# An image without feed-forward goes first, the weights' signs are made in layer 1's attention, and q is scaled where it is copied

## The chip, the cores and the metric

The kernel runs on one core of one Trainium2 chip. The metric is the device time of a launch in microseconds; the kernel before takes 2424.64 us (median of three runs, 2422.13 to 2425.38). Inside the core, TensorE (PE) multiplies matrices into PSUM, of which this kernel's pool `ps_o` has eight tiles of one bank each; VectorE (DVE), ScalarE (ACT) and GpSimd (POOL) do the rest, and SyncE (SP), ACT and POOL issue the DMAs. Every engine has its own queue of instructions.

## The reference, cut to what matters

The input is eight images of 32 x 32 positions (1024 tokens) and 384 channels, in fp32.

- Layer 0: x = x + attention(group_norm(x)) with six heads of 64. q, k and v come from one weight matrix `qkv_w`; the scores are (q/8)·k plus two relative-position terms, which are products of the unscaled q with two small tables.
- Layer 1: t = t + causal attention(layer_norm(t)), one head of 384.
- Then t = t + feed-forward(layer_norm(t)). Its weights W1 and W2 are replaced by the signs of (w - mean of w's group), in five groups, and its activations are quantised by group over the batch. With eight images and five groups the group size is 8 // 5 = 1, so images 0 to 4 have a feed-forward and for images 5, 6 and 7 that term is zero.

```
gs = n // NUM_GROUPS                       # 8 // 5 = 1
for g in range(NUM_GROUPS):                # images 0..4; the rest stay zero
    ...
Wb = Wb.at[g*gs:(g+1)*gs].set(sign(wg - wg.mean()))
```

## The kernel before, in words

`run` takes the images one after the other, 0 to 7. For each image:

- `layer0` normalises (already done), computes q and k for three pairs of heads (`project_qk`, L435; the copies out of PSUM with the bias are L462 on DVE and L464 on ACT), the relative terms (`positions`, L480 to L497: a table product, a store to DRAM and gathered loads back; `place`, L510 to L518: a split into two parts and DMAs into the tiles `f_r`), and v (`values`, L530).
- `attend0_fast` goes over three pairs p, each with 16 units of scores in six bursts of 2, 3, 3, 3, 3 and 2. A unit is two pairs of score products (L585, L589), one exponential per half (L595, ACT) and, one burst later, the product with v (L606, PE) and the running sum of the probabilities (`f_sum`, L603, DVE). When the sums of a pair are complete, two transposes and two reductions on DVE make `few` (L629, L630); in burst 2 of the next pair `divide` makes the denominators (`f_den`, L638, PE, a PSUM bank), and DVE reads them (L614, L424). In burst 1 of pair 1 the residual x is loaded (L106) and the bias added on POOL (L567).
- `attention1` has the layer norm, q (L763), v (L383) and eight chunks c of causal attention (scores L806, mask L811 on DVE, exponential L813, values L819, and L820 to L822 on DVE). The next image's group norm is done in it.
- `ffn`, for images 0 to 4, reads the sign weights from DRAM (`sign_weights`, L892 to L895, POOL's queue) and does two products (L925, L966). The first two q products of the next image are made inside it (the dictionary `ahead`). An image without feed-forward is followed at once by the next image's q products.

The first image has extra work. `load_weights` loads the weights; L136 multiplies the q part of `wqkv_sb` by 1/8 on ACT, in the queue ahead of the first group norm's square root (L343). `join_biases` (L285) and `multiply_out` (L299, copies L300 on DVE) are products made once. And the generator `binarize` makes the signs: it loads W1 and W2 in three pieces (`f_w`, L229, on POOL's queue), sums them by group (L247, DVE, 20 reductions), gets the means (L255, POOL), loads the pieces again (`f_sign`), turns each into signs (L269 and L270, DVE, 30 of each) and stores them to DRAM (L277, SP). It is advanced step by step by `next(...)`: once per burst in the first image's `attend0_fast` until the first piece's signs are done (the residual waits for that in this image), and then in its `attention1`.

The program fixes the order in which work is written down; the framework's scheduler then lays it out for each engine and may put independent instructions earlier in a queue. Buffers come from rotating pools: eleven image-sized ones (`image_`, from which `f_w` and `f_sign` are taken too), twelve pages for the probabilities, eight PSUM banks. A tile's first write waits until the earlier user of its buffer is done.

Of the kernel before, what the change touches and what calls it, by code (L numbers as in the profile page):

```python
# [31 lines left out]
QB, QEPS = 128.0, 1e-5  # L32
GSB = B // NG
B_FFN = NG * GSB
MASKED = -3.0e38
BURSTS = (2, 3, 3, 3, 3, 2)
BURSTS_AT = [sum(BURSTS[:i]) for i in range(len(BURSTS))]
# [38 lines left out]
def conv_attn_hybrid(  # L76
# [42 lines left out]
    def load_weights(pools):  # L119

        nc.scalar.dma_start(out=bqk, in_=qkv_b[0 : 2 * C].rearrange("(m p) -> p m", p=P))
        nc.vector.memset(rel, 0.0)
        for half in range(2):
            nc.scalar.dma_start(out=rel[half * HD : (half + 1) * HD, 0, : 2 * H - 1], in_=rel_hT)
            nc.scalar.dma_start(out=rel[half * HD : (half + 1) * HD, 1, : 2 * W - 1], in_=rel_wT)
        nc.scalar.dma_start(out=bv, in_=qkv_b[2 * C : 3 * C].rearrange("(m p) -> p m", p=P))
        nc.scalar.dma_start(out=b1_sb, in_=b1.rearrange("(m p) -> p m", p=P))
        src = qkv_w.rearrange("(p k) o -> p k o", k=NC)
        for i in range(3):
            nc.sync.dma_start(out=wqkv_sb[:, :, ts(i, C)], in_=src[:, :, ts(i, C)])  # L130
        nc.sync.dma_start(out=wproj_sb, in_=proj_w.rearrange("(k p) o -> p k o", p=P))
        nc.sync.dma_start(out=pb, in_=proj_b.partition_broadcast(P))
        nc.sync.dma_start(out=wv_sb, in_=wv.rearrange("(k p) o -> p k o", p=P))
        nc.sync.dma_start(out=b2_sb, in_=b2.partition_broadcast(P))

        nc.scalar.mul(wqkv_sb[:, :, 0:C], wqkv_sb[:, :, 0:C], qscale)  # L136
        nc.scalar.mul(bqk[:, 0:NPAIR], bqk[:, 0:NPAIR], qscale)
        nc.scalar.mul(rel, rel, 1.0 / qscale)
        early = pools.small.tile([P, 1], F32, tag="early", name="early_root")
        nc.scalar.activation(early, ones[:, 0:1], AF.Sqrt)  # L140
# [9 lines left out]
    )  # L150

    fold = const.tile([P, 2, 32], F32, name="fold")
    for i in range(2):
        nc.vector.tensor_reduce(fold[:, i, :], ident.rearrange("p (k i) -> p i k", k=4), AX.X, ALU.add)
    ones = const.tile([P, HD], F32, name="ones")
    nc.gpsimd.memset(ones, 1.0)

# [61 lines left out]
    def binarize(pools):  # L219

        def pieces(name):
            for n, piece in enumerate(PIECES):
                room, at = pools.flat(f"{name}_{n}"), 0
                for i, (which, src, sign, k0, k1, n_out) in enumerate(piece):
                    w = room[:, at : at + (k1 - k0) * n_out].rearrange("p (k o) -> p k o", o=n_out)
                    at += (k1 - k0) * n_out
                    nc.gpsimd.dma_start(out=w, in_=src.rearrange("(k p) o -> p k o", p=P)[:, k0:k1, :])  # L229
                    yield which, w, sign[:, k0 * n_out : k1 * n_out], n_out, i + 1 == len(piece)  # L230

        def one_ahead(loads):

            got = next(loads)
            for load in loads:
                yield got
                got = load
            yield got

        part = const.tile([P, 2, 2, NG], F32, name="sums_w")  # L240
        times = [0, 0]
        loads = one_ahead(pieces("w"))
        got = next(loads)
        yield False
        for which, w, _, n_out, _ in itertools.chain([got], loads):
            for g in range(NG):
                nc.vector.tensor_reduce(  # L247
                    part[:, times[which], which, g : g + 1], w[:, :, ts(g, n_out // NG)], AX.XY, ALU.add
                )
            times[which] += 1  # L250
            if which == 1 or w.shape[1] > 1:
                yield False
        nc.vector.tensor_tensor(part[:, 0], part[:, 0], part[:, 1], ALU.add)
        mean = const.tile([P, 2, NG], F32, name="mean_w")
        nc.gpsimd.partition_all_reduce(  # L255
            mean.rearrange("p a g -> p (a g)"), part[:, 0].rearrange("p a g -> p (a g)"), P, bass_isa.ReduceOp.add
        )
        for which, n in enumerate((FF // NG * C, C // NG * FF)):
            nc.vector.tensor_scalar_mul(mean[:, which], mean[:, which], 1.0 / n)
        done = 0  # L260
        for which, w, dst, n_out, last in one_ahead(pieces("sign")):
            gs = n_out // NG
            step = min(C // gs, w.shape[1])
            for k in range(0, w.shape[1], step):
                for g in range(NG):
                    wg, m = w[:, k : min(k + step, w.shape[1]), ts(g, gs)], mean[:, which, g : g + 1]
                    above = pools.xn.tile([P, C], F32, tag="xn", name=f"above_{which}_{n_out}")
                    above = above[:, : wg.shape[1] * gs].rearrange("p (k o) -> p k o", o=gs)
                    nc.vector.tensor_scalar(above, wg, m, None, ALU.is_gt)  # L269
                    nc.vector.scalar_tensor_tensor(wg, wg, m, above, ALU.is_lt, ALU.subtract, reverse1=True)  # L270
                    done += wg.shape[1] * gs
                    if done > 600:
                        done = 0
                        yield False
            if NG * gs < n_out:
                nc.vector.memset(w[:, :, NG * gs :], 0.0)
            nc.sync.dma_start(out=dst.bitcast(F32), in_=w.rearrange("p k o -> p (k o)"))  # L277
            if last:
                yield True
# [22 lines left out]
    def stages(pools):  # L302
# [137 lines left out]
        def layer0(b, xT):  # L440
# [9 lines left out]
            def queries_keys(m):  # L450
# [3 lines left out]
                for half, ps in enumerate(made):  # L454
                    t = ts(half, 512)
                    if m < NPAIR:
                        dst = q[:, p, t]
                    else:
                        dst = k[:, p, t].rearrange("d (g n i) -> d g i n", n=2, i=P)
                        ps = ps.rearrange("d (g i n) -> d g i n", n=2, i=P)  # L460
                    if half:
                        nc.vector.tensor_scalar_add(dst, ps, bias)  # L462
                    else:
                        nc.scalar.activation(dst, ps, AF.Identity, bias=bias)  # L464

# [68 lines left out]
            for m in range(2 * NPAIR):  # L536
# [3 lines left out]
                if m == NPAIR and unfinished:  # L540
# [1 line left out]

                    early = pools.small.tile([P, 1], F32, tag="early", name=f"early0_{b}")
                    nc.scalar.activation(early, k[:, 0, T - 1 :], AF.Exp, scale=0.0)
            if pools.fast and b == 0:
                signs.append(binarize(pools))
                next(signs[0])
            for j in range(NJ):
                values(j)
            for _ in place(0, *near[0]):  # L550
# [7 lines left out]
            later = others()  # L558
            for _ in () if pools.fast else later:
                pass  # L560
            if pools.fast and b == 0:
                join_biases(pools)

            def residual():
# [7 lines left out]
        def attend0_fast(residual, b, q, k, r, v, later):  # L572
# [90 lines left out]
            for p in range(NPAIR):  # L663
                sums = [pools.page(f"sum0_{b}_{p}_{half}") for half in range(2)]
                for n, burst in enumerate(bursts):
                    prs = [scores(p, *u) for u in burst]
                    if b == 0 and (p, n) == (0, 1):
                        multiply_out(pools)
                    for u in pending:
                        values(*u)  # L670
                    if n == 0:
                        if p > 0:
                            few = set_aside(p - 1, *last)
                        avs = [pools.o_tile(f"av0_{b}_{p}_{half}") for half in range(2)]
                    if b == 0 and xt is None and next(signs[0]) or b > 0 and (p, n) == (1, 1):
                        xt = residual()
                    if p == 0:
                        with tc.issue_after(last_exp[0]):
# [76 lines left out]
        def attention1(xt, more, b, between, start):  # L755
# [24 lines left out]
                values(j)  # L780
            for m in range(NC):
                queries(1, m)
                for work in signs:
                    next(work, None)
            for j in range(4, NJ):
                values(j)

# [5 lines left out]
        def attend1_fast(xt, b, q, xT, v, other, start):  # L793
# [33 lines left out]
            for c in range(NJ):  # L827
# [3 lines left out]
                    next(work, None)  # L831
                if c >= 2:
                    values(c - 2)
            for work in signs:
                assert next(work, None) is None
            signs.clear()
            start()
            values(NJ - 2)
            values(NJ - 1)
# [60 lines left out]
        def ffn(xt, b, gn):  # L900

            xs = [pools.halves(f"{n}_{b}", F32R) for n in ("lnT_2", "lnlo_2")]
            for half in range(2):
# [3 lines left out]
                    yield  # L907
                if half == 0 and gn is not None and pools.fast:
                    with tc.issue_after(last_transpose[0]):
                        ahead[b + 1, 0] = project_qk(b + 1, gn, 0)  # L910

            early = pools.small.tile([P, 1], F32, tag="early", name=f"early_{b}")
            nc.scalar.activation(early, rs[:, 0:1], AF.Gelu)
# [24 lines left out]
                            )  # L938
            s, _ = absmax_scale(am.rearrange("p i n -> p (i n)"), f"1_{b}")
            if gn is not None and pools.fast:  # L940
                ahead[b + 1, 1] = project_qk(b + 1, gn, 1)

# [40 lines left out]
        unfinished = []  # L985

        def run(pools):
            gn = load_T(0)
            if pools.fast:
                load_weights(pools)  # L990
            for _ in group_norm_T(0, gn):
                pass
            if pools.fast:
                make_unit(pools)
            for b in range(B):
                xt, more = layer0(b, gn)

                def between():

                    if b + 1 < B:  # L1000
                        yield from group_norm_T(b + 1)

                started = []

# [10 lines left out]
                def finish(b=b, xt=xt, add=add):  # L1015
# [1 line left out]
                        add()  # L1017
                    dst = out[b].rearrange("(j p) c -> p j c", p=P)
                    for q in range(4):
                        (nc.gpsimd if b + 1 < B else nc.sync).dma_start(  # L1020
                            out=dst[:, 2 * q : 2 * q + 2, :], in_=xt[:, 2 * q : 2 * q + 2, :]
                        )

# [52 lines left out]
```

## Time and profile before

| | |
|---|---|
| median of the three runs | 2424.64 us (2422.13 to 2425.38) |
| profiled execution, its span on the core | 2422.6 us; no other time is given for it |
| PE busy | 2378.5 us (98%) |
| DVE busy | 1392.1 us (57%) |
| ACT busy | 1035.4 us (43%) |
| POOL busy | 264.9 us (11%) |
| moved by DMA | 169.98 MB, 70 GB/s on average |

A stretch of the profile is read with the same stretch of another image beside it: all images run the same matmuls in `layer0` and `attention1`, so where the first image takes longer than the seventh, the difference is what its extra work and its waits cost. "Releaser" is what the profile gives as the end of a wait. The granted clock is TensorE's, as a share of full speed.

### The profile page before, as it was taken

What the parts mean: (1) busy time and instruction counts of PE and PEld (TensorE: products, weight loads), DVE (VectorE), ACT (ScalarE), POOL (GpSimd) and SP (SyncE); (2) the same over time, 40 slices, a digit from 0 to 9 for tenths busy, and PEclk for the clock granted to TensorE, in tenths of its full rate; (3) what the DMA queues carried; (4) which work ended last, traced back from release to release, by engine and by line L of the source; (5) the groups of instructions that cost most, each with busy time, mean ns of one, the idle gap of its engine ahead of it and who ended that gap; (6) DMA issues with size and microseconds to landing.
All of it is one profiled execution on the core that took longest, in us unless ns stands there. A gap on an engine that the chain in (4) does not pass through costs nothing.

```text
span 2422.6 us, 25725 instructions
## 1 busy us (share of the span) xinstructions
PE 2378.5 (98%) x9378; PEld 1274.1 (53%) x9378; DVE 1392.1 (57%) x2182; ACT 1035.4 (43%) x1756; POOL 264.9 (11%) x389
## 2 busy tenths in 40 slices
PE   6899999999999999999999999999999999999998
PEld 2434576445774356843458634577435543554354
DVE  4497456773466654557645577346674357525751
ACT  2352265632465513755227463246542155125520
POOL 1220001300013000032000130001300030002100
PEclk9899999999999999999999999999999999999999
DMA  7722205410127011081110631013600270018000
GB/s 196 201 96 79 78 1 121 114 53 14 39 66 170 27 40 39 1 188 64 49 39 1 131 105 65 1 39 86 149 27 1 70 165 27 0 47 161 28 1 28
DMA packets 154793, 169.98 MB, mean 70 GB/s; under 512 B 113408, under 2 KB 126048, under 8 KB 153120
## 3 DMA queue, kind: packets, MB, share of 16 engines
q1 hardware_dynamic: 134416, 98.93, 17.1%
q0 software_dynamic: 17184, 69.22, 9.6%
q8 instruction: 77, 1.26, 0.2%
q10 hardware_dynamic: 3056, 0.08, 0.1%
q14 instruction: 60, 0.49, 0.1%
HBM read 75.38 MB, written 42.47 MB: 49 GB/s over the span
## 4 chain that ended last, share of the span: by engine, by line
PE 96%; DVE 2%; DMA 1%; issue 0%; ACT 0%; POOL 0%; DVEq 0%; ACTq 0%
PE f_s L585 14%; PE f_av L606 14%; PE f_qk L435 10%; PE f_s L806 8%; PE f_av L819 8%; PE f_y L966 7%; PE f_y L925 7%; PE f_v L383 5%; PE f_v L530 5%; PE f_q L763 5%; PE f_s L589 4%; PE f_pj L383 3%; PE f_rel L480 2%; PE f_pj L693 2%; PE f_pt L311 1%; PE f_pj L698 1%
## 5 line engine op out<-in xcount | busy, mean ns | idle before, releaser
L595 ACT ACTIVATE f_pr<-f_s 128x512 f32<-128x512 f32 x768 | 412.1, 595 | 327.2 <-PE f_s L589 287.8
L585 PE MATMUL f_s<-f_q,f_k 64*128 64x512 f32 x1536 | 413.2, 609 | 10.4 <-DVE wqk L300 8.3
L603 DVE TENSOR_TENSOR f_sum<-f_sum,f_pr 128x1024 f32<-128x1024 f32 x288 | 360.8, 1300 | 18.6 <-ACT f_pr L595 18.2
L606 PE MATMUL f_av<-f_pr,f_v 128*64 128x512 f32 x1536 | 363.9, 607 | 0.0
L589 PE MATMUL f_s<-f_r,unit 64*128 64x512 f32 x768 | 309.9, 794 | 0.0
L435 PE MATMUL f_qk<-f_gnT,wqkv_sb 128*128 128x512 f32 x576 | 257.4, 600 | 8.4 <-DVE f_gnT L346 8.4
L585 PEld LDWEIGHTS f_s<-f_q,f_k 64*128 64x128 f32 x1536 | 137.9, 186 | 179.0 <-issue 105.4
L606 PEld LDWEIGHTS f_av<-f_pr,f_v 128*64 128x64 f32 x1536 | 98.9, 137 | 220.6 <-issue 194.3
L806 PE MATMUL f_s<-f_q,f_lnT 128*128 128x512 f32 (+3 forms) x576 | 195.9, 488 | 0.0
L819 PE MATMUL f_av<-f_v,f_pr 128*128 128x385 f32 x576 | 195.3, 486 | 0.0
L435 PEld LDWEIGHTS f_qk<-f_gnT,wqkv_sb 128*128 128x128 f32 x576 | 108.0, 191 | 150.0 <-issue 139.2
L813 ACT ACTIVATE f_pr<-f_s 128x512 f32<-128x512 f32 (+3 forms) x96 | 47.1, 491 | 264.1 <-DVE f_s L811 215.4
L819 PEld LDWEIGHTS f_av<-f_v,f_pr 128*128 128x128 f32 x576 | 108.2, 190 | 77.3 <-issue 11.5
L518 POOL DMA_DIRECT2D f_r<-f_far x192 | 101.2, 530 | 410.3 <-DVE f_far L511 343.5
L806 PEld LDWEIGHTS f_s<-f_q,f_lnT 128*128 128x128 f32 x576 | 102.0, 190 | 77.8 <-issue 54.1
L929 ACT ACTIVATE f_h<-f_y,b_sb 128x256 f32<-128x256 f32 x240 | 100.8, 471 | 67.5 <-PE f_y L925 67.0
L763 PE MATMUL f_q<-f_lnT,wqk 128*128 128x512 f32 x288 | 127.5, 592 | 0.0
L936 DVE TENSOR_REDUCE am<-f_h 128x1 f32<-128x1024 f32 (+2 forms) x80 | 71.6, 946 | 96.4 <-ACT f_h L929 96.4
L383 PE MATMUL f_v<-wv_sb,f_lnT 128*128 128x384 f32 x384 | 126.5, 486 | 0.0
L530 PE MATMUL f_v<-wqkv_sb,f_gnT 128*128 128x384 f32 x384 | 125.1, 486 | 0.0
L589 PEld LDWEIGHTS f_s<-f_r,unit 64*128 64x128 f32 x768 | 75.2, 187 | 91.1 <-issue 89.8
L530 PEld LDWEIGHTS f_v<-wqkv_sb,f_gnT 128*128 128x128 f32 x384 | 75.3, 196 | 50.3 <-issue 3.5
(162 smaller groups left out, 2986.2 us busy)
## 6 DMA issues: line engine op xcount, KB each, us to landing
f_far<-f_far SPq DMA_DIRECT2D x48, 512.0 KB, 3.4
f_r<-f_far POOLq DMA_DIRECT2D x192, 128.0 KB, 4.4
f_r<-f_far SPq DMA_DIRECT2D x192, 128.0 KB, 3.7
f_gnT<-in_xT SPq DMA_DIRECT2D x24, 512.0 KB, 4.7
f_x<-in_x SPq DMA_DIRECT2D x32, 384.0 KB, 5.8
out_y<-f_x POOLq DMA_DIRECT2D x28, 384.0 KB, 4.6
f_near<-f_far SPq DMA_DIRECT2D x128, 64.0 KB, 4.3
f_w1a<-w1s POOLq DMA_DIRECT2D x5, 1536.0 KB, 6.9
```

The source lines that it names most:

```text
L383: nc.tensor.matmul(ps[:, :C], xT[:, k, ts(j, P)], w[:, k, cols], start=(k == 0), stop=(k == NC - 1))
L435: nc.tensor.matmul(made[half], wqkv_sb[:, i, ts(m, P)], xT[:, i, ts(half, 512)], start=(i == 0), stop=(i == NC - 1))
L530: nc.tensor.matmul(ps, keys[:, i, j // 2, j % 2], wqkv_sb[:, i, 2 * C :], start=(i == 0), stop=(i == NC - 1))
L585: nc.tensor.matmul(sc[par], k[rows[par], p, ts(c, P)], q[rows[par], p, ts(half, 512)], start=True, stop=False)
L589: last_score[0] = nc.tensor.matmul(sc[par], unit[rows[par], c // 2 % 2].rearrange("i h w -> i (h w)"), r[2 * (c // 4) + c % 2][rows[par], ...
L595: last_exp[0] = nc.scalar.activation(pr[:, ts(par, 512)], sc[par], AF.Exp).ins
L603: nc.vector.tensor_tensor(sums[half], prev, pr, ALU.add)
L606: nc.tensor.matmul(avs[half][ts(par, HD), :], v[:, c, ts(h, HD)], pr[:, ts(par, 512)], start=(c == 0), stop=(c == NJ - 1),)
L763: nc.tensor.matmul(ps, wqk[:, k, ts(m, P)], xT[:, half, k, :], start=(k == 0), stop=(k == NC - 1))
L806: nc.tensor.matmul(sc[:, lo:], xT[:, c // 4, k, ts(c % 4, P)], q[:, half, k, lo:], start=(k == 0), stop=(k == NC - 1),)
L819: nc.tensor.matmul(av[:, : C + 1], prs[c][:, ts(j - c, P)], v[:, c, :], start=(c == 0), stop=(c == j))
L925: nc.tensor.matmul(ps, w1k[i // 2][:, ts(m, P)], xs[i % 2][:, half, i // 2, :], start=(i == 0), stop=(i == 2 * NC - 1))
```

## The change

Three edits.

1. The order of the images is 5, 0, 1, 2, 3, 4, 6, 7 (`ORDER`, with `AFTER` for the successor). All that was bound to image 0 as the first is bound to image 5; there are as many images with and without feed-forward, and the last one is still 7.
2. `binarize` starts in burst 3 of pair 2 of the first image, and is advanced two steps in each of the eight chunks of `attention1` of image 5 and then of image 0, where it must be finished. Its sums give way after every second group. The residual of the first image is loaded in burst 1 of pair 1 as in every other.
3. The weights of q are no longer multiplied by 1/8 (L136 is gone); the copies of q from PSUM multiply and add the bias in one instruction. The two reductions that make the constant `fold` (L154) are written after the first group norm.

```diff
+ORDER = (B_FFN, *range(B_FFN), *range(B_FFN + 1, B))
+AFTER = dict(zip(ORDER, ORDER[1:]))
...
-        nc.scalar.mul(wqkv_sb[:, :, 0:C], wqkv_sb[:, :, 0:C], qscale)
...
-    for i in range(2):
-        nc.vector.tensor_reduce(fold[:, i, :], ident.rearrange("p (k i) -> p i k", k=4), AX.X, ALU.add)
+
+    def make_fold():
+        for i in range(2):
+            nc.vector.tensor_reduce(fold[:, i, :], ident.rearrange("p (k i) -> p i k", k=4), AX.X, ALU.add)
...
                     part[:, times[which], which, g : g + 1], w[:, :, ts(g, n_out // NG)], AX.XY, ALU.add
                 )
+                if g % 2:
+                    yield False
             times[which] += 1
-            if which == 1 or w.shape[1] > 1:
-                yield False
...
+                    scale = qscale if m < NPAIR else 1.0
                     if half:
-                        nc.vector.tensor_scalar_add(dst, ps, bias)
+                        nc.vector.tensor_scalar(dst, ps, scale, bias, ALU.mult, ALU.add)
                     else:
-                        nc.scalar.activation(dst, ps, AF.Identity, bias=bias)
+                        nc.scalar.activation(dst, ps, AF.Identity, bias=bias, scale=scale)
...
-            if pools.fast and b == 0:
-                signs.append(binarize(pools))
-                next(signs[0])
...
-                    if b == 0 and (p, n) == (0, 1):
+                    if b == ORDER[0] and (p, n) == (0, 1):
                         multiply_out(pools)
+                    if b == ORDER[0] and (p, n) == (2, 3):
+                        signs.append(binarize(pools))
+                        next(signs[0])
...
-                    if b == 0 and xt is None and next(signs[0]) or b > 0 and (p, n) == (1, 1):
+                    if (p, n) == (1, 1):
                         xt = residual()
...
                 queries(1, m)
-                for work in signs:
-                    next(work, None)
...
-            for work in signs:
-                assert next(work, None) is None
-            signs.clear()
+            if b < B_FFN:
+                for work in signs:
+                    assert next(work, None) is None
+                signs.clear()
...
-                        ahead[b + 1, 0] = project_qk(b + 1, gn, 0)
+                        ahead[AFTER[b], 0] = project_qk(AFTER[b], gn, 0)
...
             if pools.fast:
                 make_unit(pools)
-            for b in range(B):
+                make_fold()
+            for b in ORDER:
```

The remaining lines of the diff put `ORDER[0]` and `AFTER[b]` where `0` and `b + 1` stood.

More of the change, by code (lines that the diff above doesn't have):

```diff
@@ L560, in layer0 @@
                 pass
-            if pools.fast and b == 0:
+            if pools.fast and b == ORDER[0]:
                 join_biases(pools)
@@ L940, in ffn @@
             if gn is not None and pools.fast:
-                ahead[b + 1, 1] = project_qk(b + 1, gn, 1)
+                ahead[AFTER[b], 1] = project_qk(AFTER[b], gn, 1)
             def activate(j, m0, m1):
@@ L987, in run @@
         def run(pools):
-            gn = load_T(0)
+            gn = load_T(ORDER[0])
             if pools.fast:
                 load_weights(pools)
-            for _ in group_norm_T(0, gn):
+            for _ in group_norm_T(ORDER[0], gn):
                 pass
@@ L994, in run @@
                 make_unit(pools)
-            for b in range(B):
+                make_fold()
+            for b in ORDER:
                 xt, more = layer0(b, gn)
                 def between():
-                    if b + 1 < B:
-                        yield from group_norm_T(b + 1)
+                    if b in AFTER:
+                        yield from group_norm_T(AFTER[b])
                 started = []
@@ L1019, in finish @@
                     for q in range(4):
-                        (nc.gpsimd if b + 1 < B else nc.sync).dma_start(
+                        (nc.gpsimd if b in AFTER else nc.sync).dma_start(
                             out=dst[:, 2 * q : 2 * q + 2, :], in_=xt[:, 2 * q : 2 * q + 2, :]
```

## The prediction

> **What bounds the kernel now.** I read the page's busy shares first, then a table of stretches, then the waits of the first image, then timelines.
>
> ```profile
> PE 2378.5 (98%) x9378; PEld 1274.1 (53%) x9378; DVE 1392.1 (57%) x2182; ACT 1035.4 (43%) x1756; POOL 264.9 (11%) x389
> ```
>
> PE is the bound; only its idle time and slow time can be won by moving work. The stretches (span; busy us and count of PE, PEld, DVE, ACT, POOL; granted clock, DMA share, GB/s) set the first image against image 6: the start, v to the end of layer 0's attention in images 0 and 6, and the rest of image 0.
>
> ```profile
> 0.00:21.50 21.50, 1.14 (x4) 1.00 (x4) 6.53 (x17) 4.54 (x7) 6.45 (x21) 1.00 0.91 306
> 60.50:206.50 146.00, 135.41 (x570) 55.89 (x568) 103.24 (x137) 66.34 (x111) 29.96 (x39) 0.93 0.51 145
> ...
> 206.50:305.00 98.50, 98.19 (x317) 55.80 (x318) 56.37 (x146) 19.19 (x35) 2.16 (x4) 1.00 0.18 64
> ...
> 1947.00:2064.00 117.00, 117.00 (x546) 48.95 (x545) 80.00 (x73) 64.87 (x110) 22.65 (x32) 1.00 0.36 90
> ```
>
> Image 0 takes 29.0 us longer there. Of that 8.05 us are its own products (L285 from 75.96 to 77.99, L299 from 83.65 to 89.65 in the timeline); 20.9 us are lost. The waits of 60 to 206 us name the cause:
>
> ```profile
> DVE sums_w L247 <- DMA f_w<-in_w2T: 11.2, 1, 11.2
> ...
> PE f_s L585 <- DVE wqk L300: 8.3, 1, 8.3
> ...
> PE f_s L585 <- DVE seen L424: 2.1, 1, 2.1
> ```
>
> DVE stands at a sum whose weights have not landed; the L300 copy behind it keeps a PSUM bank, and PE waits. Later DVE reaches a denominator (L424) late. After the first wait PE runs slowly:
>
> ```profile
> 102.00:113.50 11.50, 11.49 (x24) 3.45 (x24) 10.64 (x15) 3.21 (x5) 3.63 (x6) 0.50 0.52 169
> ```
>
> So the burst from 91.52 to 113.45 takes 21.93 us against 6.20 in image 6 (1969.99 to 1976.19): 15.7 lost for 8.3 idle. The one from 147.29 to 158.33 takes 11.04 against 6.19: 4.85 lost for 2.1 idle. With 0.2 before L638 this is 20.8 us.
>
> At the start, ACT's square root stands behind the weight scaling, which waits for its DMA:
>
> ```profile
> 9.03 0.20 ACT L140 ACTIVATE early_root<-ones 128x1 f32<-128x1 f32 x1
> ...
> 13.17 0.16 DVE L342 TENSOR_SCALAR gd<-f_gvar 128x1 f32<-128x1 f32 x1 [0.68 <-PE f_gvar L341]
> ...
> 19.13 1.16 ACT L136 ACTIVATE wqkv_sb<-wqkv_sb 128x1152 f32<-128x1152 f32 x1 [9.90 <-DMA wqkv_sb<-in_qkv_w]
> 20.20 0.19 ACT L343 ACTIVATE gd<-gd 128x1 f32<-128x1 f32 x1
> ...
> 21.57 12.13 PE L435 MATMUL f_qk<-f_gnT,wqkv_sb 128*128 128x512 f32 x24 [8.44 <-DVE f_gnT L346]
> ```
>
> [...] Here the first piece of `wqkv_sb`, 576 KB, took 12.4 us beside 3.15 MB of `f_w` on POOL's queue, while `f_wqkT`, 576 KB too, took 4.8 and 5.7 us later[...].
>
> **The change part by part.**
>
> *Start.* L136 goes, and so do the early `f_w` loads. L343 can run when L342 is done: 13.33, done 13.55; L344 to 13.75; L346 to PE took 0.95 (20.62 to 21.57), so PE could start near 14.7. One `fold` reduction of 0.31 leaves the queue before the aggregation: 14.3. The weight piece is issued at 6.73 and takes about 5.5 us alone: 12.3, no longer last. Gain 7.3 us. If the piece still landed at 19.1, the gain would be 2.3; the wait of 1.29 for the third chunk of `f_gnT`, partly shared with `f_w`, is all that could be added.
>
> *Q's copies.* Still 24 on DVE and 24 on ACT, with one operation more. On DVE a plain copy of 128x512 (L764) takes 689 ns and the copy with an addition (L462) 747, so I take at most 0.06 us more each; they lie beside products of 5.2 us for each m. Nothing on the path.
>
> *Image order.* In the compiled queues of PE, SP and ACT the block of one image without feed-forward stands at the front instead of near the end and nothing else changes place but L136 and the sign stores; 9378 products remain. There are as many transitions with and without feed-forward, and the last image is 7. Zero.
>
> *Signs leave image 0's layer 0.* 15 of DVE's sums, 5 more ahead of L300, 20 pairs of sign instructions and their DMAs: 20.8 us come back if nothing takes their place.
>
> *A new wait in image 5.* The scheduler has put 15 of the 20 sums directly behind pair 0's `few`, at the start of pair 1, ahead of pair 1's sums. They read `f_w` pieces whose loads stand on POOL behind the last `f_r` DMA: one 1.5 MB load, then the eight residual additions, then two loads of 768 KB. I time it from image 6, counted from its first v product (1946.9), plus the 8.05 us of own products:
>
> ```profile
> 1987.84 2.10 POOL L518 DMA_DIRECT2D f_r<-f_far  x4 [6.72 <-DVE f_far L511]
> ...
> 1992.16 8.53 POOL L567 TENSOR_TENSOR f_x<-f_x,pb 128x384 f32<-128x384 f32 x6 [0.19 <-DMA f_x<-in_x]
> ...
> 1999.14 2.30 DVE L630 TENSOR_REDUCE few<-f_tr 128x32 f32<-128x1024 f32 x2
> ...
> 2009.38 0.26 PE L638 MATMUL f_den<-few,fold 128*64 128x32 f32 x4
> ```
>
> POOL is free at 51.1, issues the big load (0.9; its 8.8 us landing, as `f_sign` of that size had, is in time), adds from 52.0 to 62.7 and issues the two others at 62.7 and 63.5. Such loads took 4.8 and 8.0 us: landed at 67.5 and 71.5. DVE ends `few` at 62.5, sums the first piece (3.65, five of L247) to 66.2, waits to 67.5, sums 2.0, waits from 69.5 to 71.5, sums 1.9 to 73.4, adds three `f_sum` (1.15 each) to 76.9, and reads the denominator by 77.4. PE makes that at 70.5 and, as at 147.05 to 150.58, needs the bank 3.5 us later: idle from 74.0 to 77.4. Between 2.1 idle for 4.85 lost and 8.3 for 15.7, 3.4 idle costs about 6.5 us. Bounds: the loads land in 4.8, or the scheduler's order does no harm, then 0 to 3.6; or the last takes 13.2, as one at the start did, then about 8.6 idle and 16 lost.
>
> *Signs in layer 1.* Image 5's attention gets five sums (3.7 us), the means and 20 pairs (about 0.88 each, 17.6); image 0's keeps 10. DVE is busy 39.7 of 97.1 us there in image 6. The sign loads are issued after L255, some 16 us after the first scores, and land near 25 (8.8): behind them the masks L811 of the last three chunks come up to 5 us late. Values lag the scores by two chunks (some 8 us) and eight banks hold five or six tiles, so I cost it at nothing; without that cover each late mask costs its lateness. SP's stores wait for the last sign of image 5, about 46 us after the first scores, and image 0's first `f_far` store is due at about 61. POOL's `out_y` and `f_r` behind the sign loads are due later still. In image 0 the last store lands about 26 us after its first scores and `f_wrest` about 34; the feed-forward starts at 54.7 (256.69 to 311.38). Zero, with up to 4 us of loss kept for the range.
>
> Sum: 2422.6 - 7.3 - 20.8 + 6.5 = 2401.0 for the profiled span. The median of the runs is 2.0 above that span, which I keep: **2403.0 us**.
>
> **Rivals.**
>
> - The new wait is covered (loads land quickly): 2396.5. For it: DMA is idle there and `f_sign` of 1.5 MB moved at 400 GB/s; against it: the additions stand ahead of two loads.
> - The new wait is as bad as the old one: 16 lost, 2412.5. For it: loads of 768 KB took up to 13.2 us; against: those shared the engines.
> - The start gives only 2.3 because `wqkv_sb` is still late: 2408. Against: the 5.5 us of `f_wqkT`.
> - Slower: DVE's in-order queue in image 5's attention. If the sign loads land over 4 us later than the 25 I assume, four masks hold up scores long enough for the banks to run out, each with an idle of about 3 us and a halved clock, 6.5 each: 26 + 6.5 - 28.1, so 2429. Against: image 0 now does 10 pairs in that layer and the stretch is as long as image 1's (98.4 us).
> - The change does not do what it says: the compiled queues show each move; only its timing is open.
>
> **How the numbers follow.** Forecast 0.52, wait covered 0.20, wait as bad as before 0.15, start late 0.07, slower 0.04, no difference left 0.02. The range 2396 to 2413 takes in the first four but for their edges. A measurement of this kernel can tell about 0.2% (4.8 us) from no change. Faster: 0.94, within: 0.02, slower: 0.04.
>
> **What would show it.** First L435 near 14.3 with the square root directly behind L342; image 5's stretch from v to its projection near 131 us instead of 146; a wait of DVE on an `f_w` DMA of 1 to 4 us and one of PE on `seen` of about 3 us, with a clock below 1 after it; `attention1` of images 5 and 0 as long as in the others. A first product later than 17, no PE wait in pair 1, or a PE wait on a mask in image 5 would make a step wrong.

## The result, and the profile after

The changed kernel takes 2397.73 us (median of four runs, 2396.02 to 2399.57), against 2424.84 for the kernel before (2422.13 to 2425.38): a ratio of 0.9892, with a 95% interval from 0.9878 to 0.9906. That is 27.1 us less, where 21.6 were forecast (2403.0, range 2396 to 2413). The profiled execution has a span of 2395.9 us and took 2397.6.

First the busy shares of the page after. PE is busy for 8.4 us less than before with the same 9378 instructions: slow products had been part of its busy time. Before, twelve products with v (L606) took 5.39 and 4.49 us behind the two pauses of the first image, where the granted clock was 0.50 from 96.5 to 113.5 and from 154.5 to 157.9 us; elsewhere such twelve take 2.79.

```profile
PE 2370.1 (99%) x9378; PEld 1272.8 (53%) x9378; DVE 1380.8 (58%) x2182; ACT 1032.9 (43%) x1755; POOL 259.5 (11%) x389
```

Then the stretches, as before (span; busy us and count of PE, PEld, DVE, ACT, POOL; granted clock, DMA share, GB/s): the start up to the first q product, image 5 from there to v, from v to its projection, and its layer 1 up to the next image's q products.

```profile
0.00:13.80 13.80, 1.14 (x4) 1.00 (x4) 6.46 (x17) 3.48 (x6) 4.28 (x18) 1.00 0.90 251
13.80:54.00 40.20, 40.20 (x96) 16.70 (x97) 14.47 (x20) 12.45 (x19) 0.70 (x1) 1.00 0.67 131
54.00:180.30 126.30, 126.03 (x569) 53.78 (x567) 86.72 (x92) 66.27 (x111) 24.81 (x36) 1.00 0.46 128
...
180.30:277.30 97.00, 96.69 (x306) 54.40 (x305) 57.25 (x151) 14.79 (x28) 4.76 (x7) 1.00 0.21 80
```

The first row was 21.57 and is 13.80. The third was 146.0 and is 126.3. The fourth holds the new work of DVE (57.25 us busy, 39.75 in image 6) and is as long as in image 6, to the hundredth: 97.00.

The PE rows of the waits after show what is left of the stalls from the start to the end of the first image's layer 0. The 8.3 us on L300 are gone, and the wait on `seen` (line 428 now) has shrunk to 0.3:

```profile
PE f_qk L439 <- DVE f_gnT L350: 1.5, 1, 1.5
PE f_gvar L345 <- DVE gd L342: 0.7, 1, 0.7
PE f_s L587 <- DVE seen L428: 0.3, 1, 0.3
```

From the starts of the first products of each stage in the two timelines, the difference comes out as follows.

| stretch | before | after | difference |
|---|---|---|---|
| start to the first q product | 21.57 | 13.80 | -7.77 |
| first q product to first v product | 38.91 | 40.22 | +1.31 |
| v to projection, first image | 145.95 | 126.30 | -19.65 |
| the rest of the span | 2216.17 | 2215.58 | -0.59 |
| span | 2422.6 | 2395.9 | -26.7 |

### The profile page after: what moved, and what is told of

Read it like the earlier page. It is cut to its first block, busy times and chain, and to the rows that moved or that the text cites. A ratio compares the mean times of both kernels' runs of the same rounds, so it can differ in the third digit from the quotient of the medians.

```text
span 2395.9 us, 25729 instructions
## 1 busy us (share of the span) xinstructions
PE 2370.1 (99%) x9378; PEld 1272.8 (53%) x9378; DVE 1380.8 (58%) x2182; ACT 1032.9 (43%) x1755; POOL 259.5 (11%) x389
## 4 chain that ended last, share of the span: by engine, by line
PE 97%; DMA 1%; DVE 1%; POOL 0%; issue 0%; DVEq 0%; ACT 0%; POOLq 0%
PE f_s L587 14%; PE f_av L608 14%; PE f_qk L439 11%; PE f_s L809 8%; PE f_av L822 8%; PE f_y L970 7%; PE f_y L929 7%; PE f_v L387 5%; PE f_v L535 5%; PE f_q L768 5%; PE f_s L591 4%; PE f_pj L387 3%; PE f_rel L485 2%; PE f_pj L698 2%; PE f_pt L315 1%; PE f_pj L703 1%
## 5 line engine op out<-in xcount | busy, mean ns | idle before, releaser
L605 DVE TENSOR_TENSOR f_sum<-f_sum,f_pr 128x1024 f32<-128x1024 f32 x288 | 348.4, 1260 | 19.2 <-ACT f_pr L597 18.8
L809 PE MATMUL f_s<-f_q,f_lnT 128*128 128x512 f32 (+3 forms) x576 | 195.9, 488 | 0.0
L809 PEld LDWEIGHTS f_s<-f_q,f_lnT 128*128 128x128 f32 x576 | 102.0, 190 | 77.8 <-issue 54.1
```

What stands on the lines that cost most here:

```text
L605: nc.vector.tensor_tensor(sums[half], prev, pr, ALU.add)
L809: nc.tensor.matmul(sc[:, lo:], xT[:, c // 4, k, ts(c % 4, P)], q[:, half, k, lo:], start=(k == 0), stop=(k == NC - 1),)
```

## Experiments

Eleven runs, all compared with the kernel before on the same chip. Times of single runs of one kernel lie 1 to 6 us apart, so most readings below are lengths of stretches in the profile, of one execution each unless the text says otherwise.

### What made the start late: the scaling or the loads

The first kernel puts the scaling of the weights back into the changed kernel; the second takes it out of the kernel before, where the early `f_w` loads stay.

```diff
 # scale_back, against the changed kernel
+        nc.scalar.mul(wqkv_sb[:, :, 0:C], wqkv_sb[:, :, 0:C], qscale)
...
-                        nc.vector.tensor_scalar(dst, ps, scale, bias, ALU.mult, ALU.add)
+                        nc.vector.tensor_scalar_add(dst, ps, bias)
...
-                        nc.scalar.activation(dst, ps, AF.Identity, bias=bias, scale=scale)
+                        nc.scalar.activation(dst, ps, AF.Identity, bias=bias)
 # q_only: edit 3 of the change alone, against the kernel before
```

> The changed kernel with the q weights scaled on ACT again, as before, and plain copies of q; all else stays. Theory 1 (the weights came late because three loads of 3.15 MB shared the DMA engines with them): with those loads gone the first piece of wqkv_sb lands near 12.5 us, the scaling ends near 13.7, the square root behind it near 13.9, and the first q product starts near 15.2, 1.4 later than the 13.80 of the changed kernel; span up by at most 1.4 us. Theory 2 (the scaling in the queue was what cost the time): the first product goes back towards 21 us and the span up by 6 to 7.

> The kernel before with the third edit alone: no scaling of the q weights, q scaled in its copies, the fold constants written after the group norm; the f_w loads stay at the start and the image order and the signs stay. Theory 1 (the loads of the signs' weights delay wqkv_sb): the weights land near 19.1 us still, the first q product starts near 19.3 instead of 21.57, span down by 2.3[...], 1 to 2.3. Theory 2 (the scaling made the delay): first product near 14.5, span down by about 6.

Measured: 2397.61 us for the first (ratio 0.9893, interval 0.9877 to 0.9910), as the changed kernel. For the second 2421.57 against 2424.18 (ratio 0.9989, 0.9982 to 0.9996). The timeline of the first, with the scaling back:

```profile
6.80 2.00 SPq L132 DMA_DIRECT2D wqkv_sb<-in_qkv_w  x3
...
12.02 1.16 ACT L138 ACTIVATE wqkv_sb<-wqkv_sb 128x1152 f32<-128x1152 f32 x1 [2.76 <-DMA wqkv_sb<-in_qkv_w]
...
13.09 0.19 ACT L348 ACTIVATE gd<-gd 128x1 f32<-128x1 f32 x1
14.47 10.88 PE L440 MATMUL f_qk<-f_gnT,wqkv_sb 128*128 128x512 f32 x18 [1.64 <-DVE f_gnT L351]
```

And of the second, without it but with the early loads:

```profile
5.35 1.47 POOL L231 DMA_DIRECT2D f_w<-in_w1T  x2
...
6.68 2.12 SPq L130 DMA_DIRECT2D wqkv_sb<-in_qkv_w  x3
...
12.84 0.20 ACT L345 ACTIVATE gd<-gd 128x1 f32<-128x1 f32 x1 [3.68 <-DVE gd L344]
...
19.64 5.85 PE L437 MATMUL f_qk<-f_gnT,wqkv_sb 128*128 128x512 f32 x7 [7.03 <-DMA wqkv_sb<-in_qkv_w]
```

The bracket at the end of a row is the idle time ahead of it and what ended it. In the first the weights are there at 12.02, 5.2 us after their issue; in the second PE itself waits 7.03 us for them, though the square root was done at 13.0. So the loads decide, as theory 1 of both texts has it: taking away the scaling alone moves the first product from 21.57 to 19.64, taking away the loads alone to 14.47, both to between 13.80 and 14.84 (six profiles of kernels with that start). The kernel with the order alone, whose start is unedited, begins at 21.02, so half a microsecond is within what executions differ by. Edit 3, which looks like the one for the start, brings less than a third of it by itself and, with edit 2 in place, nothing that these runs can tell in the time; edit 2 brings nearly all.

### What the order of the images does

The third kernel has the new order alone; the fourth has the new place of the signs alone, in the old order, where image 0's layer 1 has to hold them all.

```diff
 # order_only, against the kernel before
-            for b in range(B):
+            for b in ORDER:
...
 # signs_only, against the kernel before
+                    if b == 0 and (p, n) == (2, 3):
+                        signs.append(binarize(pools))
+                        next(signs[0])
...
-                for work in 2 * signs:
+                for work in 4 * signs:
```

> The kernel before with the image order 5, 0, 1, 2, 3, 4, 6, 7 alone; the signs are made in the first image's layer 0 as before. Forecast: nothing, 2424 us, within 2 us of the kernel before, with the same idle of PE of 8.3 and 2.1 us in the first image. Rival (the order itself brings part of the 27 us, since the first image without feed-forward is followed at once by the next): down by more than 5.

> The kernel before with the second edit alone, in the old image order: binarize starts in pair 2 of image 0, and is stepped four times per chunk in image 0's attention1, which must now hold all 30 pairs of sign instructions. Theory 1 (the placement of the signs carries the gain, the order only gives it room): layer 0 of image 0 comes down from 146 to about 126, the start gains 6 as its loads are gone, and attention1 gains 10 pairs, some 9 us of DVE, so that DVE is busy for some 70 of 97 us, and the signs are stored about 10 us before the feed-forward at best: 2400, up to 10 more where the feed-forward waits for its weights. Rival (without the new order the layer can't hold it): masks and the feed-forward's weights come late, 2410 to 2425.

Measured: 2424.43 us for the order alone, ratio 1.0003 (0.9994 to 1.0012), with both waits still there, 7.8 us on L302 and 1.8 on `seen`, where the kernel before has 8.3 and 2.1. The order alone is worth nothing, as was forecast.

The signs alone: 2414.36 us, ratio 0.9960 (0.9946 to 0.9974). Start (14.77) and layer 0 of image 0 (126.15) are as short as in the changed kernel, but image 0 takes 122.40 us from its projection to its feed-forward instead of 104.70. By its time this is the rival, but it is not the feed-forward's weights that come late: it is the masks, and the layer norm ahead of the feed-forward. Its waits between 170 and 300 us, and DVE's timeline (mask L809, signs L269 and L270, normalisation L373):

```profile
ACT f_pr L811 <- DVE f_s L809: 43.4, 7, 14.6
...
PE f_pt L311 <- DVE f_xn L373: 13.5, 2, 13.2
```

```profile
251.86 0.30 DVE L809 TENSOR_TENSOR f_s<-f_s,maskT 128x128 f32<-128x128 f32 x1 [0.82 <-PE f_s L804]
...
252.26 0.67 DVE L269 TENSOR_SCALAR above<-f_sign,mean_w 128x307 f32<-128x307 f32 x2
...
266.11 0.97 DVE L270 SCALAR_TENSOR_TENSOR f_sign<-f_sign,mean_w,above 128x304 f32<-128x304 f32 x2
...
267.08 0.29 DVE L809 TENSOR_TENSOR f_s<-f_s,maskT 128x128 f32<-128x128 f32 x1
...
281.50 1.65 DVE L373 TENSOR_SCALAR f_xn<-f_x,lmv,lrs 128x384 f32<-128x384 f32 x4
```

Between two masks there are 14.8 us of signs, DVE is behind until the last of them, and the feed-forward's layer norm stands behind them all: PE idles 13.2 us for it. A full DVE queue in layer 1 is what the forecast's slower rival rests on, and this is the one arrangement run in which it costs time: mostly in front of the layer norm, where the rival expected it at the masks. The new order spreads the signs over two such layers and gives the first of them no feed-forward. That saves 17.7 us here; without it the new place of the signs brings 10 us instead of 27. Which of the two, the spreading or the missing feed-forward, counts for how much was not run.

### What pair 1 of image 5 loses

In the changed kernel image 5 needs 126.30 us from v to projection. The next kernel orders all of `binarize`'s DVE work behind the layer norm of layer 1; it was run twice, the second time beside the changed kernel.

```diff
 # late_sums, against the changed kernel
+                last_norm[0] = nc.vector.tensor_scalar(
...
                 for work in 2 * signs:
-                    next(work, None)
+                    with tc.issue_after(last_norm[0]):
+                        next(work, None)
```

> The changed kernel with all of binarize's DVE work in image 5 and 0 ordered behind that image's layer norm, so that no sum of the weights stands in pair 1 of image 5. Theory 1 (the 1.36 us that image 5 loses in pair 1 come from those sums): the loss is gone, v to projection takes 125.0 us instead of 126.3, the means come later but attention1 has room: span down by 1.3 us. Rival (the sums, five of 0.72 and ten of 0.4 us, hold up the copies of q and v in layer 1, or the sign loads come so late that the masks or image 0's feed-forward wait): the 1.3 us come back or more, up by 1 to 5 us over the changed kernel.

> The kernel with the sums behind image 5's layer norm once more, beside the changed kernel on the same chip, since four runs did not tell their times apart. Theory 1: v to projection 124.9 again, whatever the loads do, and its time 1 to 3 us under that of the changed kernel. Rival (the sums cost elsewhere what they free in pair 1): the same time within 0.5 us, with some other stretch longer.

> The changed kernel once more, for a second profile of it and its time on the same chip as the other two. Theory 1 (the loss in pair 1 hangs on when three loads and the parts of the residual land, so it differs between executions): v to projection between 125.0 and 131.2 us, not 126.30 again, and the first q product between 13.8 and 14.9. Theory 2 (it is fixed by the order of the queues): 126.3 within 0.2.

Measured: 124.91 and 124.92 us with the late sums, within 0.1 us of the same stretch of image 6 (116.98) plus the own products (8.03 by the starts in the timeline, 8.05 in the forecast), so nothing is lost; the changed kernel's second profile has 126.14. The sums cost 1.2 to 1.4 us. In time it doesn't show: 2398.21 and 2397.91 us, against 2397.73 and 2397.38 for the changed kernel, with ranges that overlap. In the profiles the time from PE's last product (L202) to the end of the span is 9.6 and 10.1 us with the late sums and 8.8 and 9.4 without; why is open. Of the kernel with late sums, theory 1 held for the stretch and its rival for the time. Of the changed kernel, the second profile is within 0.2 us of the first, as theory 2 has it; that the loss can still change with the landing of the loads is seen only across kernels, below.

Two more kernels make DVE later still, by one and by three reductions of one page of probabilities in front of the first denominators (and a fourth `f_sum`, which the fixed order brings with it).

```diff
 # pad1 and pad3 (D = 1 and 3), against the changed kernel
+                            for i in range(D):
+                                late = nc.vector.tensor_reduce(pad[:, i : i + 1], sums[0], AX.X, ALU.add).ins
+                        with tc.issue_after(late) if late else contextlib.nullcontext():
                             divide(p - 1, few)
```

> The changed kernel with one more DVE reduction of a page (some 1.2 us) in front of the first denominators of image 5's pair 1, with the order fixed so that a fourth f_sum (1.2 us) stands ahead of them too: they are read about 2.4 us later. In the changed kernel the pause cost PE 1.36 us at full clock. Theory 1 (the forecast's rule, between 2.1 idle for 4.85 lost and 8.3 for 15.7): about 2.7 recorded idle, 5.8 lost in all, the span up by 4.4, with slow products after the pause. Theory 2[...]: 3.8 lost in all, the span up by 2.4 and no slow product.

> As the kernel with one added reduction, with three: the first denominators of image 5's pair 1 are read about 4.7 us later than in the changed kernel. The forecast's rule: about 5.0 recorded idle, 9.9 lost in all, span up by 8.5 over the changed kernel, with slow products after the pause. If pauses of this length leave the clock alone: 6.1 lost, span up by 4.7. [...]

Measured: 2401.44 us (ratio 0.9906, 0.9890 to 0.9923) and 2404.22 (0.9920, 0.9903 to 0.9937). In both PE stops for DVE, but what follows differs. PE's timeline with one reduction:

```profile
130.87 0.66 PE L587 MATMUL f_s<-f_q,f_k 64*128 64x512 f32 x1 [1.73 <-DVE seen L428]
...
132.12 2.79 PE L608 MATMUL f_av<-f_pr,f_v 128*64 128x512 f32 x12
```

And with three:

```profile
131.64 1.15 PE L587 MATMUL f_s<-f_q,f_k 64*128 64x512 f32 x2 [2.14 <-DVE seen L428]
132.18 1.05 PE L591 MATMUL f_s<-f_r,unit 64*128 64x512 f32 x1
133.15 4.16 PE L608 MATMUL f_av<-f_pr,f_v 128*64 128x512 f32 x10
```

After 1.73 us of idle twelve products with v take 2.79, as in the changed kernel from 129.47, where the granted clock is 1.00 from 126 to 140 us. After 2.14 ten of them take 4.16 (two came before the pause), 0.42 each instead of 0.23. The stretch from v to projection takes 127.72 and 131.02 us, so against the 124.91 of the kernel with late sums 2.8 us are lost in the first case and 6.1 in the second. For the first the forecast's rule gave 5.8, and 3.8 was expected with no slow product; for the second 9.9 and 6.1 were expected. Both pauses came out shorter than expected, since DVE could start on the last piece of weights 0.8 and 1.4 us earlier after v than in the changed kernel. So neither theory is right as it was put: after the first pause the products kept their speed, after the second they did not, and the 6.1 is a shorter pause with slow products, not the longer one without that was expected.

### Warming PE before its first product

The first products of image 5 take 0.85 us each, later ones 0.43. The next kernel gives PE products of `ident` to do, whose result is not used, while it waits for the group norm; the last one combines a shorter warm-up with the late sums.

```diff
 # warm, against the changed kernel; in "both": 30, 3 and 5, and the edit of late_sums
+            def warm(n):
+                ps = pools.o_tile(f"warm_{n}")
+                for _ in range(n):
+                    nc.tensor.matmul(ps[:, :P], ident, ident, start=True, stop=True)
...
+                warm(40)
             for _ in group_norm_T(ORDER[0], gn):
-                pass
+                if pools.fast:
+                    warm(3)
+            if pools.fast:
+                warm(8)
```

> The changed kernel with 51 products of ident with itself, whose result nobody reads, on PE ahead of the first group norm's products and between them. The first 24 q products took 13.4 us, the first 5.6 of them at about half speed, against 10.3 if all took 0.43. Theory 1[...]: the slow spell falls into the warm-up, the first table product comes near 24.2 instead of 27.2, span down by 3.0 us. Theory 2 (the first products are slow for their data, or the clock is bound to the time since the launch): no change, within 0.3 us. If the warm-up products run longer than planned, the group mean's product starts later than 10.4 and the start loses by the same amount.

> The changed kernel with the sums of the weights behind image 5's layer norm, and with a shorter warm-up on PE: 30 products of ident ahead of the group mean (their end is due near 10.3 us, where the 40 ended at 12.7 and held up the group mean by 2.3), 3 behind it and 5 behind the variance. If the two losses are independent: first q product between 13.8 and 14.8, at full clock, v 37.25 later, image 5 from v to its projection in 125.0: image 0's q products start near 273.5 instead of 277.3, the span is 2391 to 2393, some 3 to 4 under the changed kernel. Rival (the clock falls again in the short gaps between warm-up and first product, or the warm-up still ends late): the first 24 products take 13 us again, and only the 1.3 us of the sums are won.

Measured with 40, 3 and 8 (each shows as two records in the rows): 2397.69 us, no gain. The slow spell is gone, as theory 1 has it: from the first q product to v it takes 37.25 us, as in image 6, instead of 40.22. But the warm-up ended late, and the first product started at 15.79, which leaves 1.0. And the profiled execution (2401.82 us, the longest of four) lost 6.3 us in pair 1. Its DVE and PE rows there:

```profile
119.72 1.99 DVE L251 TENSOR_REDUCE sums_w<-f_w 128x1 f32<-128x307 f32 x5 [2.80 <-DMA f_w<-in_w1T]
123.10 1.98 DVE L251 TENSOR_REDUCE sums_w<-f_w 128x1 f32<-128x304 f32 x5 [1.38 <-DMA f_w<-in_w2T]
128.39 0.35 DVE L616 RECIPROCAL rt<-f_den 128x32 f32<-128x32 f32 x1
```

```profile
128.93 1.19 PE L587 MATMUL f_s<-f_q,f_k 64*128 64x512 f32 x1 [1.97 <-DVE seen L428]
...
131.33 4.83 PE L608 MATMUL f_av<-f_pr,f_v 128*64 128x512 f32 x12
```

Nothing in pair 1 was edited. PE came 1 us earlier, two pieces of the residual landed later (1.9 us of waiting for each on POOL), and with them the loads behind; the pause grew from 0.3 to 1.97 recorded, twelve products behind it take 4.83 us instead of 2.79, and the granted clock is 0.68 on average from 125 to 135 us. This is the kind of wait that was forecast, at nearly the loss that was forecast (6.5).

With both edits: 2395.6 us (2395.05 to 2396.41; ratio 0.9881, 0.9864 to 0.9897), against 2397.38 (2396.45 to 2399.82; 0.9890, 0.9874 to 0.9907) for the changed kernel beside it: 1.8 us less, the four runs of each don't overlap, the intervals of the ratios do. PE's timeline of its start:

```profile
1.78 9.71 PE L998 MATMUL f_warm<-ident 128*128 128x128 f32 x60 [1.78 <-POOL ident masks.py:199]
11.33 0.28 PE L337 MATMUL f_gmean<-gmv,over_group 128*128 128x1 f32 x2
11.47 0.91 PE L998 MATMUL f_warm<-ident 128*128 128x128 f32 x6
12.31 0.38 PE L345 MATMUL f_gvar<-gd,over_group 128*128 128x1 f32 x2
12.55 1.36 PE L998 MATMUL f_warm<-ident 128*128 128x128 f32 x10
14.22 7.99 PE L441 MATMUL f_qk<-f_gnT,wqkv_sb 128*128 128x512 f32 x18 [0.31 <-DVE f_gnT L350]
```

Image 5's projection starts at 176.49 instead of 179.09 in the changed kernel's profile of the same set, as expected; image 0's q products start at 273.50, where 273.5 was expected. The span is 2393.7 where 2391 to 2393 was expected, since the end behind the last product takes 10.6 us here. This kernel's median is the lowest of all versions run.

## Why the prediction was right, point by point

- **Start, -7.3 forecast, -7.8 measured.** First product forecast at 14.3, measured at 13.80 and, over six profiles, 13.80 to 14.84. The weight piece landed in 5.2 us once the `f_w` loads were gone, with 5.5 estimated. Missing from the sum: the first products are slow, for a time that differs between executions. They were so before too (38.91 us from q to v, 37.25 in image 6); after, the same stretch is 1.3 us longer in the first profile and 0.0 to 1.5 over the six. The earlier start is not the cause: the changed kernel's second profile starts at 14.03 and takes 38.92, the kernel with the order alone starts at 21.02 and takes 39.94.
- **Image 0's layer 0, -20.8 forecast.** Confirmed: against 124.91 as the length without a loss, the kernel before lost 21.0.
- **A new wait in image 5, +6.5 forecast, +1.4 measured.** This is the term that was mis-sized. It accounts for the 5.1 us between the forecast span (2401.0) and the measured one (2395.9), because the other misses happen to cancel: -0.5 at the start, +1.3 in the slow products, -0.2 in layer 0, -0.6 in the rest. The queue order, DVE's waits for the two small loads and the wait on `seen` came as described. DVE also waited 0.64 for the big load, which took 11.2 us instead of 8.8, and the slow clock that was to follow the wait on `seen` did not come: it is 1.00 from 126 to 140 us. These are DVE's rows after:

```profile
114.47 3.59 DVE L251 TENSOR_REDUCE sums_w<-f_w 128x1 f32<-128x614 f32 x5 [0.64 <-DMA f_w<-in_w1T]
119.39 1.99 DVE L251 TENSOR_REDUCE sums_w<-f_w 128x1 f32<-128x307 f32 x5 [1.33 <-DMA f_w<-in_w1T]
122.37 1.98 DVE L251 TENSOR_REDUCE sums_w<-f_w 128x1 f32<-128x304 f32 x5 [1.00 <-DMA f_w<-in_w2T]
...
127.67 0.35 DVE L616 RECIPROCAL rt<-f_den 128x32 f32<-128x32 f32 x1
```

  Counted from the first v product at 54.0, the step that failed is "counted from its first v product, plus the 8.05 us of own products". PE is shifted by that (L640 at 124.45, 70.5 forecast, 70.4 measured), POOL and DVE are shifted by less: POOL is free at 49.2 instead of 51.1, `few` is done at 59.8 instead of 62.5. So the two loads were issued 1.9 and 2.2 us earlier, landed at 65.3 and 68.3 instead of 67.5 and 71.5 (for the last, 2.2 us from the issue and 1.0 from a quicker landing), and the denominators were read 3.4 us earlier. The second half of the step, "between 2.1 idle for 4.85 lost and 8.3 for 15.7", failed too: on record a pause of 1.73 cost 2.8, one of 1.97 cost 6.3 and one of 2.08 cost 4.85, which no such line gives.
- **Signs in layer 1, 0 forecast.** Confirmed: 97.01 us from image 5's projection to the next q product, 97.00 in image 6, which has no signs; and in image 0, which makes the other 10 pairs, 104.70 us from its projection to its feed-forward, as before. Signs and masks alternate on DVE there; the last sign store was issued 41 us after the first scores, 46 forecast.
- **Image order, 0.** Confirmed by the run with the order alone, 1.0003 (0.9994 to 1.0012).
- **Q's copies, 0.** A q copy on DVE takes 748 ns on average with the multiplication, 747 without, and on ACT 680 in both; 0.06 us more was the bound.
- **The total.** The measured 2397.73 is nearer the rival of a covered wait (2396.5) than the forecast (2403.0). That wait was nearly covered, less for the reason given (quick loads, 1.0 us of it) than because POOL issued the loads earlier (2.2 us). How near the edge this is shows in the kernel with the long warm-up, where the same wait cost 6.3. A full DVE queue in layer 1, the slower rival's ground, is real, as the kernel with the signs alone shows; the new order is what keeps it away.

## What to carry to other kernels

A large load that nobody needs soon can still cost if it is issued beside the first small one that everybody needs, here 5 to 7 us of the start: look at what shares the DMA engines with the first weights before blaming the instruction that waits for them. Move deferred work to where its engine has room and no deadline follows: the same 30 sign pairs cost nothing spread over two layers and 17.7 us in one. When times of another image are shifted to price a stage, shift each engine by its own waits, not all by PE's, and price a PE pause twice, with the products behind it at their usual speed and with slow ones, here twelve of them in 2.79 us or in 4.3 to 4.8.

## What was not expected of the hardware

- Pauses of nearly the same length were followed by products at different speeds. Behind the wait on `seen` in pair 1 of the first image, twelve products with v took 2.79 us after recorded pauses of 0.27 (the changed kernel) and 1.73 (one added reduction), but 4.33 after 1.79 (the order alone), 4.83 after 1.97 (the long warm-up), 4.49 after 2.08 (the kernel before) and 4.76 after 2.64 (edit 3 alone); ten took 4.16 after 2.14 (three added reductions). The pauses of 1.73 and 1.79 us are 0.06 apart. The granted clock fell in those stretches: it is 0.83 on average over 150 to 160 us in the kernel before and over 148 to 158 in the one with the order alone, and 0.68 over 125 to 135 with the long warm-up.
- Where the clock fell against its pause, and for how long, differed too. In the kernel before it is 0.50 from 96.5 us, 2.7 us after PE's idle of 8.3 began, to 113.5, and again from 154.5, 1.8 us after the pause of 2.08 had ended, to 157.9: spells of 17.1 and 3.4 us. The runs don't separate the length of a pause from where it falls.
- Recorded idle is shorter than the loss even where the products behind it kept their speed: 0.27 for 1.4 and 1.73 for 2.8, and the kernel with the scaling back lost 0.95 us there with no idle recorded. Over six profiles of five kernels with the sums in this place, DVE started on the last piece of weights 66.9 to 70.1 us after the first v product. That may be a part of why executions of one kernel differ by several us, but only one kernel of these has two profiles, and they lost 1.4 and 1.2 us, so this is not shown.
- At the start PE's first products of 128x512 took 0.85 instead of 0.43 us, for about 3.2 us (before) to 5.8 us (after). The rows give a granted clock of 1.00 for that time as well (20 to 28 us before, 14 to 20 after), so what made them slow is not shown. Behind products on a constant, made during the wait for the first data, it was gone in both kernels that had them: 37.25 and 37.35 us from the first q product to v.
